# Inverting the chunk matrix of delta attention on diagonal tiles of the PE array

## The chip, the core and the metric

The kernel runs on one core of a Trainium2 chip, in one launch. The metric is device time in microseconds (us). The core's engines work at the same time, each in the order of its own queue: TensorE (PE, matmuls, with PEld for the loading of weights), VectorE (DVE), ScalarE (ACT), GpSimd (POOL) and SyncE (SP), whose queue issues the DMAs. Matmul results arrive in PSUM and must be copied out by DVE or ACT.

## What is computed

The reference is two transformer layers on 2 x 1,024 tokens of width 512, all in float32. The part that matters here is the attention of the first layer, a gated delta rule with 6 heads of 64:

```python
def step(S, inputs):
    q_t, k_t, v_t, g_t, b_t = inputs
    S = S * jnp.exp(g_t)[..., None, None]
    kv = jnp.einsum('bhk,bhkv->bhv', k_t, S)
    u = b_t[..., None] * (v_t - kv)
    S = S + jnp.einsum('bhk,bhv->bhkv', k_t, u)
    o_t = jnp.einsum('bhk,bhkv->bhv', q_t * scale, S)
    return (S, o_t)
```

The kernel doesn't run this step by step. It takes the tokens in chunks of 128. Inside a chunk the updates `u` of all 128 tokens solve a triangular system, one per head: a 128x128 matrix with ones on its diagonal, which holds the weighted products of the keys. The kernel inverts this matrix for each chunk and head. There are 8 chunks per batch, so 16 inversions of 6 matrices each. After the attention come an MLP with 4-bit weights, a second attention and a second MLP with 2:4 sparsity.

## The kernel before

The class `Delta` does the first attention. Batch 0 runs in `first`, batch 1 in `second`. For each chunk there are four streams of instructions, written as Python generators; each `yield` ends a step.

- `prepare(c)` (6 steps) makes the keys, the decay and the matrix. It keeps the matrix transposed as `AT` (128 partitions x 6 heads x 128). At its end `gather` (L603, L605) sends the eight 16x16 blocks on the diagonal to DRAM and back as one tile of 48 x 16 x 16.
- `solve(c)` (5 steps) inverts these 48 blocks on DVE, row by row (L617, L618). ACT turns the result round (L621). Two DMAs (L625) write both forms to DRAM, and twelve DMAs read them back: eight of 16x16 blocks (for 6 heads) into `X16` (L628), four into `T16` (L631), the transposed form of the even blocks.
- `invert(c)` (8 steps) makes the whole inverse `X` out of the small ones by doubling: with the two diagonal blocks of a pair inverted, the block off the diagonal is minus one inverse times the block of the matrix times the other inverse. It goes from 16 to 32 to 64 to 128. In the first two levels each head is one 128x128 matmul, with everything off the blocks zero: the product with `AT` (L644), a masking by `signs` into `mix` on DVE (L646), the product of `mix` and `X` (L654), an ACT copy (L656). `mix` holds the identity in its odd blocks. Then the transposed even blocks are needed for the next level; PE makes them by a transpose (L661 after level one, L670 after level two), and ACT copies them into `Te` (L663, L672). The last level takes two products of 64x64 tiles (L676, L682), whose results DVE moves (L678, L683).
- `advance(c)` (7 steps) uses `X` and the state: it computes `u` (L703), the output and the next state, and ends with a transpose (oT, L758) and the output projection (out_ps or, in the second batch, small_ps at L201).

In `first` each slot of the loop has 24 ticks. A stream gets a length and a range of ticks, and its steps are spread evenly over them. In one slot run `advance` of a chunk, `invert` of the next, `solve` of the one after that, `prepare` of the third, and the projections of later chunks, in this program order within a tick.

In `second` a slot runs three streams together: `normed`, `late` (`invert`, then `advance` of chunk slot - 1) and `early` (`prepare` of chunk slot, two empty steps, `solve`). Each round takes one step of each stream that is not yet done and yields `fill`, 3.3 us. For every yield `weave` puts in steps of the first MLP (`mlp[0].rest()`, lines L1042 and L201 with o_ps) until their nominal 3.4 us each have used up what is due. What is left of the MLP when `second` ends runs after it without interruption. So a slot lasts as many rounds as its longest stream needs, and one more in which the streams are found to be over.

The order of PE, DVE, ACT and POOL is the program's order, under `tc.manual_schedule`. The order of SP, and so of the DMA issues, is not among the engines listed there.

PSUM has three pools: `one` (two tiles of one bank), `two` (two tiles of two banks, called `wide` here) and `acc` (two single banks, taken in turn by `small`). `AT`, `X`, `Te`, `mix` have one buffer each, except `AT` with three (first batch) or two; `X16` and `T16` have one.

```python
streams = [normed(slot - 2), late(slot - 1), early(slot)]
while streams:
    streams = [f for f in streams if next(f, self) is not self]
    yield fill
```

Of the kernel before, what the change touches and what calls it, by code (L numbers as in the profile page):

```python
# [26 lines left out]
F32 = mybir.dt.float32  # L27
# [4 lines left out]
ALU = mybir.AluOpType  # L32
# [4 lines left out]
P = 128  # L37
# [5 lines left out]
NH, DH = 6, 64  # L43
# [109 lines left out]
def bc(ap, shape):  # L153
    return ap.to_broadcast(shape)
# [94 lines left out]
SB = 16  # L249
# [4 lines left out]
class Delta:  # L254
# [36 lines left out]
    def tools(self):  # L291

        core, nc, a = self.core, self.core.nc, self.a
        wp = core.pools("d_w")
        self.wo = wp.tile([P, NG, DM], F32, name="wo0")
        nc.sync.dma_start(out=self.wo, in_=a["wo0"])

        self.upper = wp.tile([P, P], F32, name="upper")
        nc.gpsimd.memset(self.upper, 1.0)
        nc.gpsimd.affine_select(  # L300
            out=self.upper, in_=self.upper, pattern=[[1, P]], compare_op=ALU.is_ge, fill=0.0, base=0,
            channel_multiplier=-1,
        )
        self.ones = wp.tile([P, P], F32, name="ones")
        nc.gpsimd.memset(self.ones, 1.0)


        self.signs, self.mix = {}, {}
        for w in (SB, 2 * SB):
            n = P // (2 * w)  # L310
            sg = wp.tile([P, n, w], F32, tag=f"signs{w}", name="signs")
            nc.gpsimd.memset(sg, -1.0)
            for pattern, base, mult in (
                ([[-2 * w, n], [0, w]], -w, 1),
                ([[2 * w, n], [0, w]], 2 * w - 1, -1),
            ):
                nc.gpsimd.affine_select(
                    out=sg, in_=sg, pattern=pattern, compare_op=ALU.is_ge, fill=0.0, base=base,
                    channel_multiplier=mult,
                )  # L320
            nc.gpsimd.affine_select(
                out=sg, in_=sg, pattern=[[-2 * w, n], [-1, w]], compare_op=ALU.not_equal, fill=1.0, base=0,
                channel_multiplier=1,
            )
            self.signs[w] = sg
            m = wp.tile([P, NH, P], F32, tag=f"mix{w}", name="mix")
            nc.gpsimd.tensor_copy(m, bc(core.ident[:, None, :], [P, NH, P]))
            self.mix[w] = m

        self.X16 = wp.tile([P, NH, P], F32, name="X16")  # L330
        nc.gpsimd.memset(self.X16, 0.0)
        self.T16 = wp.tile([P, NH, P // 2], F32, name="T16")
# [154 lines left out]
    def prepare(self, c):  # L487
# [79 lines left out]
        pT = self.ring("pT", [P, NH, P], keep)  # L567
        AT = self.ring("AT", [P, NH, P], deep)
        spots = [self.wide() for _ in range(2)]
        for m in range(NG):  # L570
            for r in range(2):
# [7 lines left out]
                )  # L579
        for i, t in ((1, AT), (0, pT)):  # L580
            for k, ps in enumerate(spots):
# [26 lines left out]
    def solve(self, c):  # L608

        nc, d, inv = self.core.nc, self.d[c], self.inv  # L610
        blk = d.pop("blk")
        n = NB * NH
        turned = inv.rearrange("b s u -> b u s")
        for rows in (range(1, 7), range(7, 11), range(11, 14), range(14, 16)):
            for t in rows:
                prod = self.ring("prod", [n, SB * SB], 1)[:, : t * t].rearrange("b (u s) -> b u s", u=t)
                nc.vector.tensor_mul(prod, turned[:, :t, :t], bc(blk[:, None, :t, t], [n, t, t]))  # L617
                nc.vector.tensor_reduce(inv[:, t, :t], prod, AX.X, ALU.add, negate=True)  # L618
            yield
        invT = self.ring("prod", [n, SB * SB], 1).rearrange("b (s t) -> b s t", s=SB)  # L620
        nc.scalar.copy(invT, turned)  # L621
        names = [f"d{x}{self.b}_{c}" for x in "TX"]
        away = [self.core.tc.dram_tile([NB, NH, SB, SB], F32, name=x) for x in names]
        for t, dst in zip((inv, invT), away):
            nc.sync.dma_start(out=dst.rearrange("n h s t -> (n h) s t"), in_=t)  # L625
        for i in range(NB):
            rows = slice(i * SB, (i + 1) * SB)
            nc.sync.dma_start(out=self.X16[rows, :, rows], in_=away[1][i].rearrange("h s t -> s h t"))  # L628
            if i % 2 == 0:
                cols = slice(i // 2 * SB, (i // 2 + 1) * SB)  # L630
                nc.sync.dma_start(out=self.T16[rows, :, cols], in_=away[0][i].rearrange("h s t -> s h t"))  # L631
        yield

    def invert(self, c):


        nc, ident, d = self.core.nc, self.core.ident, self.d[c]
        AT = d.pop("AT")
        hw = P // 2
        X, Te = self.X16, self.T16  # L640
        for w in (SB, 2 * SB):
            ps = self.small()
            for h in range(NH):
                nc.tensor.matmul(ps[:, h * hw : (h + 1) * hw], AT[:, h, :], Te[:, h, :], start=True, stop=True)  # L644
            mix = self.mix[w]
            nc.vector.tensor_mul(  # L646
                mix.rearrange("p h (i two c) -> p h i two c", two=2, c=w)[:, :, :, 0, :],
                ps[:, : NH * hw].rearrange("p (h i c) -> p h i c", h=NH, c=w),
                bc(self.signs[w][:, None, :, :], [P, NH, hw // w, w]),
            )  # L650
            yield
            ps = self.wide()
            for h in range(NH):
                nc.tensor.matmul(ps[:, h * P : (h + 1) * P], mix[:, h, :], X[:, h, :], start=True, stop=True)  # L654
            X = self.ring("X32", [P, NH, P], 1) if w == SB else self.ring("X", [P, NH, P], 1)
            nc.scalar.copy(X.rearrange("p h t -> p (h t)"), ps[:, : NH * P])  # L656
            yield
            if w == SB:
                ps = self.wide()
                for h in range(NH):  # L660
                    nc.tensor.transpose(ps[:, h * P : (h + 1) * P], X[:, h, :], ident)  # L661
                Te = self.ring("Te", [P, NH, hw], 1)
                nc.scalar.copy(  # L663
                    Te.rearrange("p h (i c) -> p h i c", c=2 * w),
                    ps[:, : NH * P].rearrange("p (h i two c) -> p h i two c", two=2, c=2 * w, h=NH)[:, :, :, 0, :],
                )
            else:
                ps = self.small()
                for h in range(NH):
                    nc.tensor.transpose(ps[:hw, h * hw : (h + 1) * hw], X[:hw, h, :hw], ident[:hw, :hw])  # L670
                Te = self.ring("Te", [P, NH, hw], 1)[:hw]
                nc.scalar.copy(Te.rearrange("p h t -> p (h t)"), ps[:hw, : NH * hw])  # L672
            yield
        ps = self.small()
        for h in range(NH):
            nc.tensor.matmul(ps[hw:, h * hw : (h + 1) * hw], AT[:hw, h, hw:], Te[:, h, :], start=True, stop=True)  # L676
        Y = self.ring("Te", [P, NH, hw], 1)
        nc.vector.tensor_scalar_mul(Y[hw:].rearrange("p h t -> p (h t)"), ps[hw:, : NH * hw], -1.0)  # L678
        yield
        ps = self.small()  # L680
        for h in range(NH):
            nc.tensor.matmul(ps[:hw, h * hw : (h + 1) * hw], Y[hw:, h, :], X[hw:, h, hw:], start=True, stop=True)  # L682
        nc.vector.tensor_copy(X[:hw, :, hw:], ps[:hw, : NH * hw].rearrange("p (h t) -> p h t", h=NH))  # L683
        d["X"] = X
        yield

# [82 lines left out]
    def first(self, xT, weights, mlp):  # L769
# [3 lines left out]
        core, nc, banks, a = self.core, self.core.nc, self.banks, self.a  # L773
# [4 lines left out]
        n = 2  # L778
# [24 lines left out]
        for slot in range(-ahead, CH + 1):  # L803
            streams = []

            def add(stream, length, start=0, end=24):
                streams.append([stream, length, 0, start, end])
# [9 lines left out]
            f = slot + ahead  # L817
# [1385 lines left out]
```

## Time and profile before

| | us |
|---|---|
| three runs | 3,094.76, 3,098.05, 3,098.5; median 3,098.05 |
| the profiled execution's own time | 3,102.61 |
| its span, from the first instruction to the last | 3,100.6 |
| granted PE clock, mean | 0.990 |

| stretch | what runs | PE, DVE, ACT busy us of 100 |
|---|---|---|
| 100 to 200 us | first batch of the delta attention, projections of the second | 92.47, 78.78, 56.82 |
| 300 to 400 us | the same, later, with the first MLP | 94.72, 64.71, 40.72 |
| 400 to 500 us | end of the first batch, first MLP | 98.11, 30.64, 14.22 |
| 600 to 700 us | second batch of the delta attention, first MLP | 97.17, 65.50, 23.76 |
| 1,100 to 1,200 us | its end and the rest of the first MLP | 97.72, 50.79, 15.89 |

Rows of `invert` in the trace, each x16 chunks: L644 makes 24 records per chunk (384 in all), L654 24, L661 6, L670 6, L676 12, L682 12. On DVE: L646 at 550 ns twice per chunk, L678 560, L683 543. On ACT: L656 at 799 ns twice, L663 480, L672 472.

How to read it: a line of the page gives line, engine, operation, what it writes and reads, shapes, count, then busy us in all and mean ns of one. A matmul's form `64*64 64x64` is rows and columns of the array in use, then partitions and elements of what streams through. One f32 matmul call makes two MATMUL records. The busy time of overlapping records counts once in the sum, so the sum divided by the count can be below the duration of one. In the chain of waits each piece has its start, its length, and what PE or another engine did in it; the start of the next piece is the end of this one.

### The profile page before, as it was taken

The numbers are of one execution on the slowest core, as the hardware profiler recorded it, in microseconds if no ns is written. First come the engines' busy times: TensorE is split into PE (matmuls) and PEld (weight loads), VectorE is DVE, ScalarE is ACT, GpSimd is POOL, SyncE is SP. The second block draws the span as 40 slices with busy tenths as digits, with TensorE's granted clock in tenths as the row PEclk, the third lists the DMA queues.
The fourth block names the chain that finished last, engine by engine and source line by source line (L and its number), as shares of the span: only waits on it lengthen the run. The fifth ranks groups of instructions, "written<-read, shape, count | busy, mean of one in ns | idle before, by whom it ended". The sixth has DMA issues, their size and how long they took to land.

```text
span 3100.6 us, 35161 instructions
## 1 busy us (share of the span) xinstructions
PE 3016.1 (97%) x12652; PEld 1583.6 (51%) x12652; DVE 1914.2 (62%) x3554; ACT 961.1 (31%) x1488; POOL 697.5 (22%) x772
## 2 busy tenths in 40 slices
PE   8999999999999999999999999999999999999998
PEld 6777754555555554545435444446433243234547
DVE  6788633565666544477567656745675577354767
ACT  6654311222222211211462125522113511532221
POOL 2223101122222212465221221222002500530000
PEclk9999999999999999999999999999999999999999
DMA  4232313233232225155111110141010010024211
GB/s 138 66 85 66 100 44 111 65 97 98 98 96 82 91 93 171 52 184 199 36 50 63 51 62 26 36 146 58 24 41 1 31 51 14 1 94 144 83 37 51
DMA packets 196525, 235.36 MB, mean 76 GB/s; under 512 B 53952, under 2 KB 148672, under 8 KB 195840
## 3 DMA queue, kind: packets, MB, share of 16 engines
q1 hardware_dynamic: 196352, 233.12, 23.3%
q8 instruction: 100, 1.64, 0.2%
q14 instruction: 73, 0.60, 0.1%
HBM read 160.42 MB, written 72.61 MB: 75 GB/s over the span
## 4 chain that ended last, share of the span: by engine, by line
PE 80%; DVE 9%; POOL 3%; issue 3%; DMA 2%; ACT 1%; SPq 0%; DVEq 0%; POOLq 0%; ACTq 0%
PE z_ps L1042 24%; PE o_ps L201 12%; PE z_ps L1088 8%; PE u_ps L201 5%; PE g_ps L201 5%; PE st_ps L1605 5%; PE av_ps L1636 4%; PE s_ps L1547 4%; DVE cv L475 2%; PE proj_ps L201 1%; DVE prod L617 1%; PE wide_ps L654 1%; PE small_ps L644 1%; PE den_ps L1658 1%; DVE inv L618 1%
## 5 line engine op out<-in xcount | busy, mean ns | idle before, releaser
L1015 ACT COPY part<-z_ps 128x512 f32<-128x512 f32 x288 | 168.7, 586 | 722.4 <-PE z_ps L1042 494.6
L1042 PE MATMUL z_ps<-xT,z_left 128*128 128x512 f32 x768 | 359.4, 597 | 0.1
L1556 DVE TENSOR_REDUCE top<-s_ps 128x2 f32<-128x1024 f32 x256 | 300.9, 1217 | 76.3 <-PE s_ps L1547 76.2
L1042 PE MATMUL z_ps<-xt,z_left 128*128 128x512 f32 x576 | 274.2, 598 | 2.2 <-issue 1.0
L1616 ACT ACTIVATE es<-st_ps 128x1024 f32<-128x1024 f32 x214 | 209.9, 1022 | 125.6 <-PE st_ps L1605 120.4
L1042 PEld LDWEIGHTS z_ps<-xT,z_left 128*128 128x128 f32 x768 | 141.4, 190 | 186.8 <-issue 161.7
L201 PE MATMUL o_ps<-w_down,h 128*128 128x512 f32 x512 | 230.1, 598 | 0.6 <-DVE part L1076 0.6
L1042 PE MATMUL z_ps<-xT,w_left 128*128 128x512 f32 x384 | 180.8, 600 | 4.7 <-DVE part L1076 2.4
L1076 DVE TENSOR_TENSOR part<-z_ps,part 128x512 f32<-128x512 f32 x108 | 74.4, 689 | 178.6 <-PE z_ps L1042 172.9
L1042 PEld LDWEIGHTS z_ps<-xt,z_left 128*128 128x128 f32 x576 | 106.0, 190 | 146.8 <-issue 124.0
L1651 POOL TENSOR_TENSOR es<-es 128x512 f32<-128x512 f32 x96 | 132.6, 1409 | 143.6 <-PE av_ps L1636 139.9
L1605 PE MATMUL st_ps<-q,kT 17*128 17x512 f32 x1024 | 160.1, 650 | 1.8 <-ACT es L1616 1.8
L1547 PE MATMUL s_ps<-kT,q 16*128 16x512 f32 x1024 | 153.9, 640 | 4.9 <-DVE top L1556 4.8
L201 PEld LDWEIGHTS o_ps<-w_down,h 128*128 128x128 f32 x512 | 94.8, 191 | 108.1 <-issue 104.2
L201 PE MATMUL proj_ps<-xT,wqkv 128*128 128x256 f32 x576 | 135.5, 390 | 8.4 <-ACT raw L459 6.7
L1636 PE MATMUL av_ps<-es,v 128*32 128x512 f32 x1024 | 139.2, 615 | 0.0
L1042 PE MATMUL z_ps<-xt,w_left 128*128 128x512 f32 x288 | 136.4, 596 | 1.6 <-DVE part L1076 1.6
L1678 DVE TENSOR_TENSOR acc<-acc,es 128x1024 f32<-128x1024 f32 x96 | 131.8, 1420 | 0.0
L1077 POOL TENSOR_TENSOR h<-h,part 128x512 f32<-128x512 f32 x48 | 66.5, 1388 | 278.9 <-DVE part L1076 278.9
L201 PEld LDWEIGHTS proj_ps<-xT,wqkv 128*128 128x128 f32 x576 | 109.8, 195 | 27.2 <-ACT raw L459 8.9
L1060 DVE TENSOR_TENSOR h<-z_ps,part 128x512 f32<-128x512 f32 x84 | 57.9, 689 | 103.8 <-PE z_ps L1042 90.5
L1206 DVE TENSOR_TENSOR x<-x,o_ps 128x512 f32<-128x512 f32 x64 | 43.8, 685 | 120.0 <-PE o_ps L201 119.8
(317 smaller groups left out, 5177.6 us busy)
## 6 DMA issues: line engine op xcount, KB each, us to landing
sums<-factor SPq DMA_DIRECT2D x24, 512.0 KB, 3.3
kept_gate<-w_left SPq DMA_DIRECT2D x12, 896.0 KB, 3.8
kept_up<-w_left SPq DMA_DIRECT2D x12, 896.0 KB, 3.9
z_left<-kept_gate SPq DMA_DIRECT2D x12, 896.0 KB, 4.6
z_left<-kept_up SPq DMA_DIRECT2D x12, 896.0 KB, 4.6
wd<-kept_down SPq DMA_DIRECT2D x16, 512.0 KB, 4.5
xl<-park SPq DMA_DIRECT2D x32, 256.0 KB, 3.4
z_left<-sums SPq DMA_DIRECT2D x16, 512.0 KB, 4.1
```

What stands on the lines that cost most here:

```text
L201: nc.tensor.matmul(ps, lhsT, rhs, start=(i == 0), stop=(i == len(pairs) - 1))
L1015: self.core.nc.scalar.copy(t, src)
L1042: self.core.nc.tensor.matmul(ps, left[l][:, k, :], self.right[r][:, k, :], start=(first and k == 0), stop=(k == 1), skip_group_check=True,)
L1076: nc.vector.tensor_add(v, ps, v)
L1088: nc.tensor.matmul(ps[:, i * dm : (i + 1) * dm], left[l][:, k, i * P : (i + 1) * P], right[r][k], start=(first and i == 0 and k == 0), sto ...
L1547: nc.tensor.matmul(tiles[h4 // 2][:, h4 % 2 * 512 : h4 % 2 * 512 + 512], q1s[t][r : r + HALF, gr, :], kT[r : r + HALF, gr, j * 512 : (j + ...
L1556: nc.vector.tensor_reduce(top[:, j, h : h + 2], tiles[e].rearrange("p (i k) -> p i k", i=2), AX.X, ALU.max, negate=True)
L1605: nc.tensor.matmul(tiles[h4 // 2][h4 % 2], kT[r : r + CR, gr, kt * P : (kt + 1) * P], q2[r : r + CR, gr, :], start=True, stop=True,)
L1616: nc.scalar.activation(t.rearrange("p i q -> p (i q)"), tile[2], AF.Exp, scale=HALF**-0.5)
L1636: nc.tensor.matmul(av[gr][32 * h4 : 32 * h4 + 32, :], v[:, kt, 4 * gr + h4, :], es[u][h4 // 2][:, h4 % 2, :], start=(kt == 0), stop=(kt == ...
L1651: eng.tensor_add(t, t, es[u][h4 // 2][:, h4 % 2, :])
L1678: nc.vector.tensor_add(t, es[u - 1][e] if kt == 1 else t, es[u][e])
```

## The change

`invert` is rewritten in six steps, and works on diagonal tiles of the array instead of full 128x128 products. At the first level the low half (partitions 0 to 63) and the high half (64 to 127) are separate 64x64 matmuls, on 64 columns of a compact `X16` (128 x 6 x 64). At the second level only the 32x32 blocks that are not known yet are computed, on 32x32 tiles. The transposed forms are no longer made by PE transposes: the same product is computed again with its two operands exchanged (`pt` beside `ps`). `X` is one of two tiles taken in turn, with its lower left quarter set to zero once; the copies write only the blocks. `solve` loads into the compact tiles, with the same twelve DMAs. The set-up in `tools` keeps one `signs` and one `mix` of 64 columns in place of two of 128. In `first`, the stream's length goes from 8 to 6.

```diff
+        self.Xs = [wp.tile([P, NH, P], F32, name=f"X{i}") for i in range(2)]
+        for X in self.Xs:
+            nc.gpsimd.memset(X[hw:, :, :hw], 0.0)
...
-            nc.sync.dma_start(out=self.X16[rows, :, rows], in_=away[1][i].rearrange("h s t -> s h t"))
+            cols = slice(i % 4 * SB, (i % 4 + 1) * SB)
+            nc.sync.dma_start(out=self.X16[rows, :, cols], in_=away[1][i].rearrange("h s t -> s h t"))
             if i % 2 == 0:
-                cols = slice(i // 2 * SB, (i // 2 + 1) * SB)
+                cols = slice(i % 4 // 2 * SB, (i % 4 // 2 + 1) * SB)
                 nc.sync.dma_start(out=self.T16[rows, :, cols], in_=away[0][i].rearrange("h s t -> s h t"))
...
+        ps = heads(self.small()[:, : NH * qw])
         for h in range(NH):
+            for part in halves:
+                nc.tensor.matmul(ps[part, h, :], AT[part, h, part], self.T16[part, h, :], start=True, stop=True)
+        mix = self.mix
+        nc.vector.tensor_mul(
+            mix.rearrange("p h (i two c) -> p h i two c", two=2, c=SB)[:, :, :, 0, :],
+            ps.rearrange("p h (i c) -> p h i c", c=SB),
+            bc(self.signs[:, None, :, :], [P, NH, 2, SB]),
+        )
         yield
+        wide = self.wide()
+        ps, pt = (heads(wide[:, o : o + NH * hw]) for o in (0, 512))
         for h in range(NH):
+            for part in halves:
+                nc.tensor.matmul(ps[part, h, :], mix[part, h, :], X16[part, h, :], start=True, stop=True)
+        for h in range(NH):
+            for part in halves:
+                nc.tensor.matmul(pt[part, h, :], X16[part, h, :], mix[part, h, :], start=True, stop=True)
+        for part in halves:
+            nc.scalar.copy(X[part, :, part], ps[part])
+        Te = self.ring("Te", [P, NH, hw], 1)
+        nc.scalar.copy(Te, pt)
+        yield
+        ps = heads(self.small()[:, : NH * qw])
+        for h in range(NH):
+            for p in range(2):
+                e, o = quarters[2 * p : 2 * p + 2]
+                nc.tensor.matmul(ps[o, h, :], AT[e, h, o], Te[e, h, :qw], start=True, stop=True)
+        Z = self.ring("Z", [P, NH, qw], 1)
+        for o in quarters[1::2]:
+            nc.vector.tensor_scalar_mul(Z[o], ps[o], -1.0)
+        yield
+        ps = heads(self.small()[:, : NH * qw])
+        pt = heads(self.small()[:, : NH * qw])
+        for h in range(NH):
+            for p in range(2):
+                e, o = quarters[2 * p : 2 * p + 2]
+                nc.tensor.matmul(ps[e, h, :], Z[o, h, :], X[o, h, o], start=True, stop=True)
+        o = quarters[1]
+        for h in range(NH):
+            nc.tensor.matmul(pt[o, h, :], X[o, h, o], Z[o, h, :], start=True, stop=True)
+        for p in range(2):
+            e, o = quarters[2 * p : 2 * p + 2]
+            nc.scalar.copy(X[e, :, o], ps[e])
+        o = quarters[1]
+        nc.scalar.copy(Te[o, :, :qw], pt[o])
+        yield
+        ps = heads(self.small()[:, : NH * hw])
+        for h in range(NH):
+            nc.tensor.matmul(ps[high, h, :], AT[low, h, high], Te[low, h, :], start=True, stop=True)
+        Y = self.ring("Y", [P, NH, hw], 1)
+        nc.vector.tensor_scalar_mul(Y[high], ps[high], -1.0)
+        yield
+        ps = heads(self.small()[:, : NH * hw])
+        for h in range(NH):
+            nc.tensor.matmul(ps[low, h, :], Y[high, h, :], X[high, h, high], start=True, stop=True)
+        nc.vector.tensor_copy(X[low, :, high], ps[low])
         d["X"] = X
         yield
...
             if 0 <= slot + 1 < CH:
-                add(self.invert(slot + 1), 8, 4)
+                add(self.invert(slot + 1), 6, 4)
```

Here `low` and `high` are the two halves of the partitions, `quarters` the four quarters, `hw` is 64, `qw` 32, and `SB` 16.

More of the change, by code (lines that the diff above doesn't have):

```diff
@@ L305, in tools @@
         nc.gpsimd.memset(self.ones, 1.0)
[L308 to L320, printed above, removed]
+        hw = P // 2
@@ L321, in tools @@
+        sg = wp.tile([P, 4, SB], F32, name="signs")
+        nc.gpsimd.memset(sg, -1.0)
+        for pattern, base, mult in (
+            ([[-2 * SB, 4], [0, SB]], -SB, 1),
+            ([[2 * SB, 4], [0, SB]], 2 * SB - 1, -1),
+        ):
             nc.gpsimd.affine_select(
-                out=sg, in_=sg, pattern=[[-2 * w, n], [-1, w]], compare_op=ALU.not_equal, fill=1.0, base=0,
-                channel_multiplier=1,
-            )
-            self.signs[w] = sg
-            m = wp.tile([P, NH, P], F32, tag=f"mix{w}", name="mix")
@@ L327, in tools @@
-            nc.gpsimd.tensor_copy(m, bc(core.ident[:, None, :], [P, NH, P]))
-            self.mix[w] = m
-        self.X16 = wp.tile([P, NH, P], F32, name="X16")
+                out=sg, in_=sg, pattern=pattern, compare_op=ALU.is_ge, fill=0.0, base=base, channel_multiplier=mult
+            )
+        nc.gpsimd.affine_select(
+            out=sg, in_=sg, pattern=[[-2 * SB, 4], [-1, SB]], compare_op=ALU.not_equal, fill=1.0, base=0,
+            channel_multiplier=1,
+        )
+        self.signs = wp.tile([P, 2, SB], F32, name="signs_half")
@@ L331, in tools @@
+        self.mix = wp.tile([P, NH, hw], F32, name="mix")
+        for p in range(2):
+            rows = slice(p * hw, (p + 1) * hw)
+            nc.gpsimd.tensor_copy(self.signs[rows], sg[rows, 2 * p : 2 * p + 2])
+            nc.gpsimd.tensor_copy(self.mix[rows], bc(core.ident[rows, None, rows], [hw, NH, hw]))
+        self.X16 = wp.tile([P, NH, hw], F32, name="X16")
         nc.gpsimd.memset(self.X16, 0.0)
-        self.T16 = wp.tile([P, NH, P // 2], F32, name="T16")
+        self.T16 = wp.tile([P, NH, 2 * SB], F32, name="T16")
@@ L634, in invert @@
     def invert(self, c):
[L637 to L673, printed above, removed]
@@ L674, in invert @@
-        ps = self.small()
-        for h in range(NH):
-            nc.tensor.matmul(ps[hw:, h * hw : (h + 1) * hw], AT[:hw, h, hw:], Te[:, h, :], start=True, stop=True)
-        Y = self.ring("Te", [P, NH, hw], 1)
-        nc.vector.tensor_scalar_mul(Y[hw:].rearrange("p h t -> p (h t)"), ps[hw:, : NH * hw], -1.0)
+        nc, d = self.core.nc, self.d[c]
+        AT, X, X16 = d.pop("AT"), self.Xs[c % 2], self.X16
+        hw, qw = P // 2, P // 4
+        low, high = slice(0, hw), slice(hw, P)
+        halves = (low, high)
@@ new lines, in invert, with heads @@
+        quarters = [slice(i * qw, (i + 1) * qw) for i in range(4)]
+        def heads(ap):
+            return ap.rearrange("p (h t) -> p h t", h=NH)
+        ps = heads(self.small()[:, : NH * qw])
+        for h in range(NH):
+            for part in halves:
[5 more added lines that the diff above has]
+            bc(self.signs[:, None, :, :], [P, NH, 2, SB]),
+        )
@@ L679, in invert @@
         yield
-        ps = self.small()
+        wide = self.wide()
+        ps, pt = (heads(wide[:, o : o + NH * hw]) for o in (0, 512))
         for h in range(NH):
-            nc.tensor.matmul(ps[:hw, h * hw : (h + 1) * hw], Y[hw:, h, :], X[hw:, h, hw:], start=True, stop=True)
-        nc.vector.tensor_copy(X[:hw, :, hw:], ps[:hw, : NH * hw].rearrange("p (h t) -> p h t", h=NH))
+            for part in halves:
+                nc.tensor.matmul(ps[part, h, :], mix[part, h, :], X16[part, h, :], start=True, stop=True)
@@ new lines, in invert @@
+        for p in range(2):
+            e, o = quarters[2 * p : 2 * p + 2]
[9 more added lines that the diff above has]
+        yield
```

## The prediction

> **What bounds the kernel now.** I read the page's busy line first, then busy time by windows, then the chain of waits piece by piece for the two stretches in which `invert` runs (chunks 0 to 7 of the first batch, its L644 rows from 112 to 428 us, and of the second, 545 to 1,128 us).
>
> ```profile
> PE 3016.1 (97%) x12652; PEld 1583.6 (51%) x12652; DVE 1914.2 (62%) x3554; ACT 961.1 (31%) x1488; POOL 697.5 (22%) x772
> ```
> ```profile
> 200.00:300.00 100.00, 93.79 (x570) 74.41 (x569) 84.07 (x236) 51.70 (x98) 26.14 (x32) 1.00 0.25 69
> ...
> 700.00:800.00 100.00, 97.76 (x405) 55.58 (x404) 58.21 (x127) 28.03 (x48) 24.08 (x27) 1.00 0.32 105
> ```
> The first figures behind the window are busy us of PE, PEld, DVE, ACT, POOL. From 200 to 300 us DVE is nearly as full as PE; from 700 to 800 us only PE is. The chain's pieces, added by engine, say the same: from 100 to 300 us 94 us are DVE and 42 PE; from 300 to 450 us 120 of 150 are PE; from 500 to 1,150 us 572 of 650 are PE. So a us of PE work is worth a us in the second batch, about that in the last three chunks of the first, and little before them.
>
> **What `invert` costs now.** One chunk in the chain, between matmul blocks of eight 128x512 records:
>
> ```profile
> 1103.92 3.43 PE o_ps L201 x8
> 1107.35 1.28 PE small_ps L644 x12
> 1108.64 3.49 PE o_ps L201 x8
> ...
> 1116.90 0.45 PE small_ps L670 x6
> 1117.35 3.63 PE o_ps L201 x8
> 1120.98 0.84 PE small_ps L676 x12
> ```
> The reader is to see two things. One f32 matmul makes two records, a transpose one. And a block of eight takes 3.43 us beside full-array work but 3.63 between two visits to 64x64 tiles (L670, L676), so a visit costs 0.20 us beside its own 0.84: PE pays for changing the tile size. The starts of L676's records lie 58 ns apart, 0.70 for twelve. Per chunk: L644 twice 2.56, L654 twice 2.68, L661 0.66 (1.34 and 0.66 in the same view), L670 0.45 + 0.20, L676 and L682 1.04 each. Sum **8.63 us**, 138 us for 16 chunks.
>
> **What it costs after.** Six visits, all on small tiles: 24, 48, 24, 36, 12 and 12 records, 156 for 84. One after another, at 58 ns for a 64-column record (L676) and about half, 30 ns, for a 32-column one (an estimate by columns; bounds 15 and 58) plus 0.34 for each visit (1.04 - 0.70): 1.73 + 3.12 + 1.06 + 1.42 + 1.04 + 1.04 = 9.41. That is 0.8 more than now. The change pays only if the records of the low and the high half, which alternate in program order, run side by side. The trace of before has no pair of diagonal tiles, but neighbours:
>
> ```profile
> 573.42 0.47 PE L670 MATMUL small_ps<-ident,X 64*64 64x64 f32 x5
> 573.67 0.48 PE L573 MATMUL wide_ps<-tmp,qkT 64*128 64x256 f32 x1
> 573.72 0.22 PE L670 MATMUL small_ps<-ident,X 64*64 64x64 f32 x1
> 573.78 1.51 PE L573 MATMUL wide_ps<-tmp,qkT 64*128 64x256 f32 x11
> ```
> ```profile
> L1636 PE MATMUL av_ps<-es,v 128*32 128x512 f32 x1024 | 139.2, 615 | 0.0
> ```
> L573 alternates between the two row halves: 12 records of 256 columns take 1.5 us, where 16 records of the same width on the full array (L201 proj_ps, 228.05 to 231.71 in the chain) take 3.66, so twelve would take 2.75. It runs in pairs. Its first record even starts before the last L670: the other row half goes ahead. L1636 puts four column tiles into one PSUM bank: 139.2 / 1,024 = 0.14 us a record of 512 columns, against 0.43 (3.43 / 8) on the full array. So pairs by rows and by columns both work, and I take the pair on the diagonal at full overlap: 24 x 0.029 + 0.34 = 1.04; 48: 1.73; 24 of 32 columns in pairs 0.36 + 0.34 = 0.70; 36, of which 24 pair, 0.72 + 0.34 = 1.06; then 1.04 twice. Sum **6.61**, 2.0 less per chunk: 16 us in each batch where PE binds. Bounds: 9.41 with no overlap; with it 6.1 and 7.6 for the two ends of the 32-column record.
>
> The Trainium skill speaks against it: "TensorEngine Tiling (Array Packing)", Gotcha 1, says that different row tiles can't use one PSUM bank at the same time, and here low and high share a bank (on other partitions). L573 keeps its halves in separate banks, so no row here refutes it for row tiles; L1636 does for column tiles. By the rule the sum would be 9.41, by the rows 6.61.
>
> Evictions. DVE: two of 128x384 (0.55 each, L646) become one of 128x192 and two of 32x192 (0.35 each, an estimate from L730, 64x192 at 348 ns); L678 and L683 stay: 2.2 us before, 2.15 after. ACT: two of 0.80 (L656), 0.48 and 0.47 become three of about 0.47 (L672's shape) and three of about 0.3: 2.55 to 2.3. Nothing gained or lost on DVE where it binds. POOL's set-up shrinks by some 3 us, at 2 to 7 us and 465 to 488 us, beside PE work: nothing. X gets a second buffer: I find no wait on it, nothing.
>
> **The price that the diff doesn't show.** `invert` yields six times, not eight. In the first batch its steps are only spread wider over the same 24 ticks. In the second a slot lasts as many rounds as its longest stream: 8 + 7 + 1 = 16 now, 14 after, as `early` (6 + 2 + 5 yields) needs 14 too. Each round brings one block of MLP matmuls; those that go come back after the last slot (the MLP runs on to 1,200 us), so they cost nothing. But they cover the way of `solve`'s result through DRAM. `solve` sends its blocks in round 13; the next slot's round 1 reads T16:
>
> ```profile
> 608.39 7.13 PE z_ps L1042 x16
> 615.52 0.33 PE small_ps L758 x3
> 615.85 3.44 PE z_ps L1042 x8
> 619.29 2.58 PE small_ps L201 x6
> 621.86 6.87 PE z_ps L1042 x16
> 628.73 1.28 PE small_ps L644 x12
> ```
> ```profile
> 616.34 0.37 SPq L625 DMA_DIRECT2D dT<-inv  x1
> ...
> 623.36 0.43 SPq L631 DMA_DIRECT2D T<-dT  x1
> ```
> ACT's copy (L621) ends at 612.95 and L644 starts 15.6 us later. After the change oT and out_ps (0.33 + 2.58) lie ahead of that copy and two blocks (6.87) are gone: 15.6 - 9.8 = 5.8 us remain. The last T16 load is issued at 623.36 and lands 1.6 later (median of L631), at about 625 = copy + 12. L644, with every later PE instruction and their DVE and ACT readers queued behind it, would wait some 6 us. In chunk 9 SP is held up by eight L938 loads before L625. The other chunks, by the same rows (gap left; T16 landed, after the copy): chunk 10 5.5; 11.5. 11 8.7; 7.3. 12 6.6; 15.5 (SP held by kept_gate and seven L938). 13 3.8; 8.3. 14 6.9; 7.2. 15 6.3; 6.7. Waits 6 + 6 + 0 + 9 + 4.5 + 0.3 + 0.4 = **26 us** if SP's order stays. Chunk 8 already has only two blocks there (5.4 us) and doesn't wait, because SP sends the four T16 loads ahead of X16: landed 4 us after the copy; that order in all slots costs **0**. SP's queue isn't in the hand-written order, so the order after is open. I take a prompt queue with mixed loads, the nearest to chunks 11, 14 and 15: T16 at copy + 7.5, against gaps of 3.8 to 8.7: about 2 us x 7 = **14**.
>
> **Sum.** Second batch -16 + 14 = -2. First batch: 2.0 for the last three chunks, and a quarter of it (the part of `invert` that lies on the chain there, 9 of some 43 us) for five: -6 - 2 = -8; bounds 0 and -16. Together **-10 us**. The profiled execution took 3,102.6 us (span 3,100.6), 4.6 above the median of 3,098.05; I take the difference off the median: **3,088 us**.
>
> **Rivals.**
> 1. Forecast, chance 0.38: pairs overlap, T16 comes about 2 us late in seven slots. -10, from -17 to -4; own range 3,081 to 3,094.
> 2. T16 in time, 0.27: SP sends T16 first, as for chunk 8. -16 - 8 = -24: **3,074**; with all of the first batch's 16, 3,066. For: that slot has the same two blocks. Against: in six of the other seven slots a load of X16 or several lie between.
> 3. T16 as late as now, 0.17: -24 + 26 = +2: **3,100**; slower as soon as waits pass 30 us, 4.3 per slot. For: SP waits 47 us for DVE w_left at L934 between 590 and 1,140 us. Against: two of those delays are rows of MLP loads, which become fewer per slot.
> 4. The slower one, 0.18: low and high don't overlap. Place: the first four visits. Price: 9.41 - 8.63 = 0.8 per chunk, 6 in the second batch and some 3 in the first, plus the 14 of T16: +23, **3,121**. Without T16's wait it decides where less than 0.28 of the overlap comes (0.8 / 2.8). Against it stand L573 and L1636. That the change doesn't do what it says is this case.
>
> About 0.2% (6 us) is what a measurement of this kernel can tell from no change. Faster by more: 0.33 of case 1 and case 2, 0.60. Within: 0.05 of case 1, 0.13 of case 3, 0.18. Slower: 0.04 of case 3, case 4, 0.22. The range leaves out half of case 4 and the fringe of 2: **3,070 to 3,114**.
>
> **What would show it.** In the timeline, low and high records of step 1 starting within some 10 ns and the 24 ending within about 0.8 us (right), or 1.4 (case 4). Step 2 in about 1.5 us. A block between two visits still at 3.63. In the waits of PE after 590 us, step 1 waiting for T or a semaphore for about 2 us per slot (case 1), none (2) or 4 and more (3). L573 and L676 unchanged. Slots of 68 instead of 77 us. The forecast is wrong most easily in SP's order, which I can't read from before, and in how much of the first batch DVE paces.

## The result, and the profile after

The changed kernel takes 3,126.66 us (median of five runs, 3,122.35 to 3,129.11), against 3,098.05 before: a ratio of 1.0091, interval 1.0077 to 1.0105. It is 28.6 us **slower**; the forecast was 10 us faster, and the time lies above the range. The profiled execution took 3,122.35 us (span 3,120.3), the fastest of the five, so the two profiles differ by 19.7 us and not by 28.6.

Line numbers have moved. In the new kernel `solve` is L619 and L620 on DVE, its copy on ACT L623, its loads L631 and L634; the six steps of `invert` start at L653, L665 (with L668), L678, L688 (with L691), L700 and L706; oT is L782 (758 before), fed by R (L778); the MLP's blocks are L1066 and o_ps at L201. The line of busy time on the page:

```profile
PE 3000.9 (96%) x13804; PEld 1544.1 (49%) x13804; DVE 1920.9 (62%) x3570; ACT 958.8 (31%) x1520; POOL 696.3 (22%) x772
```

PE is busy 15 us less than before (3,016.1), in a longer span. So the work did shrink, and PE waits more. By windows (busy us of PE, PEld, DVE, ACT, POOL with counts, then granted clock, DMA share, GB/s):

```profile
200.00:300.00 100.00, 93.19 (x767) 71.65 (x766) 83.86 (x239) 55.00 (x108) 26.80 (x31) 0.98 0.20 57
...
600.00:700.00 100.00, 85.79 (x400) 45.66 (x400) 56.03 (x125) 22.54 (x41) 19.43 (x24) 0.90 0.29 90
700.00:800.00 100.00, 93.10 (x581) 51.82 (x582) 58.37 (x128) 30.48 (x57) 24.86 (x29) 0.98 0.33 107
```

From 600 to 700 us PE was busy 97.17 us before and is now busy 85.79, at a clock of 0.90. The steps of `invert` themselves are as short as forecast. In the chain of waits, one chunk:

```profile
855.05 0.84 PE wide_ps L665 x24
855.89 0.70 PE wide_ps L668 x24
...
863.66 0.50 PE small_ps L678 x24
864.16 3.63 PE z_ps L1066 x8
```

Step 2's 48 records take 1.54 us, step 3's 24 take 0.50, and the block behind a visit to small tiles takes 3.63 as before. What PE now waits for, in the view of waits from 540 to 1,140 us (us in all, times, longest), starts with two lines of which the view of before has none:

```profile
PE small_ps L653 <- DMA T<-dT: 18.2, 7, 6.4
PE small_ps L782 <- DVE R L778: 10.7, 4, 4.6
```

The first is the wait for T16 that the prediction priced at 14 us: seven waits, in five of the seven slots. The second is oT, the end of `advance`, which waits for DVE. The chain from 815 to 852 us shows both in one slot:

```profile
830.27 0.77 DVE prod L619
831.07 0.25 DVE inv L620
831.32 0.59 DVE x L1230
831.91 0.85 DVE R L778
832.76 0.14 issue
832.90 0.88 PE small_ps L782 x3
833.77 5.57 PE o_ps L201 x8
...
847.79 1.70 DMA T<-dT
849.49 0.14 issue
849.62 0.85 PE small_ps L653 x22
```

R stands in DVE's queue behind rows of `solve` and the MLP's own work (x); PE stood idle for 4.58 us ahead of L782, and the block behind it took 5.57 us instead of 3.43, as the granted clock was 0.5 from 831 to 838 us. Before, the same place is PE alone, as the prediction's lines from 608 to 630 us show. Two rounds fewer per slot move `advance` up against `solve`: its last steps, oT and the output projection (before in rounds 14 and 15, behind all of `solve`), now fall into rounds 12 and 13, and R into round 11, while `solve` does its rows in rounds 9 to 12.

They also bring the end of `solve` closer to the next `invert`. T16 is read from dT, and dT is written from `inv`, DVE's own result; only dX needs ACT's copy. So T16's way begins with DVE's last row. By the timelines, in the seven slots from 590 us on that row (L620) ends 8.3 to 12.6 us before L653's turn comes, on average 10.4; in e1 below it is 13.8 to 19.3, on average 17.1. The 6.7 us between them are about the two blocks that went (6.87).

The other part is SP's queue. Nearly half of the 18.2 us (6.39 and 2.46) lies in one slot, at 620 us, where the last row had ended 12.6 us ahead:

```profile
613.88 0.43 SPq L627 DMA_DIRECT2D dT<-inv  x1
614.41 0.37 SPq L627 DMA_DIRECT2D dX<-prod  x1
614.83 0.42 SPq L882 DMA_DIRECT2D gw<-gw  x1
621.95 0.35 SPq L958 DMA_DIRECT2D codes<-in_pk_down  x1
...
622.87 0.38 SPq L634 DMA_DIRECT2D T<-dT  x1
```

SP issues dT late, behind loads for the MLP, and then stands for 6.6 us at L958, a load of MLP codes that waits for DVE; the loads of T16 stand behind it. Such waits are longer than before. SP's own waits from 590 to 1,140 us, first before, then after:

```profile
SPq L934 <- DVE w_left L953: 47.0, 8, 12.9
```
```profile
SPq L958 <- DVE w_left L977: 85.1, 12, 14.0
```

The balance closes with PE alone. The stretch is from chunk 8's first matmul of `invert` to the first matmul of the second attention (lat_ps). "Half clock" is the time in which the granted clock is 0.5.

| kernel | stretch, us | PE busy | PE waits | half clock |
|---|---|---|---|---|
| before | 692.3 | 674.7 | 17.4 | 10.2 |
| after | 721.3 | 671.3 | 50.2 | 47.8 |
| e1, two empty steps between `invert` and `advance` | 678.5 | 656.0 | 22.2 | 6.8 |
| e2, two empty steps behind `advance` | 694.9 | 662.6 | 32.2 | 24 |
| e3, before with `solve` two steps later | 734.5 | 686.9 | 47.4 | 51 |
| e9, one empty step ahead of `invert`, one behind | 667.7 | 651.9 | 15.8 | 10.2 |

Waits grow by 32.8 us. Busy time falls by only 3.4, though e1, with the same matmuls, is busy 18.7 less than before: the other 15.3 us are nearly all the same work at half the clock, at which PE worked 35.2 us here and 6.8 in e1.

The stretch grew by 29.0 us, more than the 19.7 between the two profiles. Chunk 8 starts 5.9 us earlier after the change (540.0 against 545.9 us), and what follows the stretch is 3.4 us shorter. The earlier start is no finding: among the profiles of kernels with the same first batch it lies between 540.0 and 546.4.

How a stall costs twice is seen in windows of 3.4 us:

```profile
619.80:623.20 3.40, 0.00 (x0) 0.00 (x0) 3.00 (x7) 0.00 (x0) 0.19 (x1) 0.96 0.03 11
623.20:626.60 3.40, 0.39 (x2) 0.28 (x2) 0.00 (x0) 0.00 (x0) 1.21 (x2) 0.50 0.33 79
626.60:630.00 3.40, 1.15 (x21) 1.19 (x22) 0.00 (x0) 0.00 (x0) 0.00 (x0) 0.50 0.16 29
630.00:633.40 3.40, 3.40 (x16) 2.71 (x14) 1.31 (x3) 0.81 (x1) 0.00 (x0) 0.54 0.18 57
```

PE waits at L653 from 619.6 to 626.0 us. In the window without any work the granted clock (third figure from the end) is still near 1; then it drops to 0.5 and stays there through the first window that is full again, 630 to 633.4, whose work is done at about half speed.

### The profile page after: what moved, and what is told of

It reads as the page before. It is cut to its first block, busy times and chain, and to the rows that moved or that the text cites. A ratio compares the mean times of both kernels' runs of the same rounds, so it can differ in the third digit from the quotient of the medians.

```text
span 3120.3 us, 37545 instructions
## 1 busy us (share of the span) xinstructions
PE 3000.9 (96%) x13804; PEld 1544.1 (49%) x13804; DVE 1920.9 (62%) x3570; ACT 958.8 (31%) x1520; POOL 696.3 (22%) x772
## 4 chain that ended last, share of the span: by engine, by line
PE 79%; DVE 11%; DMA 3%; issue 2%; POOL 2%; SPq 1%; ACT 1%; DVEq 0%; POOLq 0%; ACTq 0%
PE z_ps L1066 24%; PE o_ps L201 11%; PE z_ps L1112 8%; PE u_ps L201 5%; PE g_ps L201 5%; PE st_ps L1629 5%; PE s_ps L1571 4%; PE av_ps L1660 4%; DVE cv L477 2%; DVE prod L619 1%; DVE inv L620 1%; PE den_ps L1682 1%; PE proj_ps L201 1%; PE hT_ps L1474 1%; PE wide_ps L527 1%
## 5 line engine op out<-in xcount | busy, mean ns | idle before, releaser
L1066 PE MATMUL z_ps<-xT,z_left 128*128 128x512 f32 x768 | 359.3, 597 | 0.1
L1066 PE MATMUL z_ps<-xt,z_left 128*128 128x512 f32 x576 | 274.2, 598 | 2.2 <-issue 1.0
L201 PE MATMUL o_ps<-w_down,h 128*128 128x512 f32 x512 | 233.8, 608 | 1.8 <-DVE x L1230 1.0
L1066 PEld LDWEIGHTS z_ps<-xT,z_left 128*128 128x128 f32 x768 | 141.4, 190 | 186.8 <-issue 161.7
L1066 PE MATMUL z_ps<-xT,w_left 128*128 128x512 f32 x384 | 181.8, 603 | 7.7 <-DVE h L1084 3.1
L1066 PEld LDWEIGHTS z_ps<-xt,z_left 128*128 128x128 f32 x576 | 106.0, 190 | 146.8 <-issue 124.1
L201 PEld LDWEIGHTS o_ps<-w_down,h 128*128 128x128 f32 x512 | 97.2, 195 | 116.1 <-issue 110.2
L1066 PE MATMUL z_ps<-xt,w_left 128*128 128x512 f32 x288 | 140.5, 611 | 3.8 <-DVE part L1100 2.7
L201 PE MATMUL proj_ps<-xT,wqkv 128*128 128x256 f32 x576 | 137.0, 391 | 7.4 <-ACT raw L461 7.3
L1702 DVE TENSOR_TENSOR acc<-acc,es 128x1024 f32<-128x1024 f32 x96 | 131.8, 1420 | 0.0
L201 PEld LDWEIGHTS proj_ps<-xT,wqkv 128*128 128x128 f32 x576 | 109.0, 194 | 27.7 <-ACT raw L461 10.9
```

What stands on the lines that cost most here:

```text
L201: nc.tensor.matmul(ps, lhsT, rhs, start=(i == 0), stop=(i == len(pairs) - 1))
L1066: self.core.nc.tensor.matmul(ps, left[l][:, k, :], self.right[r][:, k, :], start=(first and k == 0), stop=(k == 1), skip_group_check=True,)
L1702: nc.vector.tensor_add(t, es[u - 1][e] if kt == 1 else t, es[u][e])
```

## The experiments

Theory A is the place: two rounds fewer per slot bring the end of `advance` onto DVE beside `solve`'s rows, and `solve`'s end close to the next `invert`. Its rivals are that one of these two does it alone (the load of T16, or the meeting on DVE), and that the narrow matmuls themselves cost more than their rows show. Unless it is said otherwise an edit is one of the changed kernel, in `second`.

**e1: the two rounds given back, between `invert` and `advance`.**

```diff
                 yield from self.invert(c)
+                yield
+                yield
                 yield from self.advance(c, keep)
```

> The changed kernel with two empty steps between invert and advance in the second batch, so that a slot again lasts 16 rounds and advance, solve and the loads of T16 stand to each other as before. Theory A (the loss comes from the two rounds that are gone: T16 late, and waits of PE for DVE at the oT transpose, each with half-clock windows behind it): PE waits for T16 near 0, the second batch is 16 us faster than before, 3,070 to 3,082 in all, granted clock back to 0.99. Theory B (the narrow tiles themselves lower the granted clock, or cost PE more than their records show): clock stays near 0.98, 3,105 or more.

3,080.13 us beside 3,099.83 for the kernel before: ratio 0.9938 (0.9925 to 0.9950), 19.7 us faster. The chain of e1 at the same place of a slot, a slot later, is PE without a gap:

```profile
917.48 0.33 PE small_ps L782 x3
...
922.11 6.87 PE z_ps L1068 x16
928.97 0.82 PE small_ps L653 x24
```

So the narrow tiles pay, and the whole loss and more (48 us between e1 and after, each against the kernel before) is the place.

**e2: the two rounds given back behind `advance`.** `solve`'s result gets its cover of two blocks again, but the end of `advance` still meets `solve`'s rows.

```diff
                 yield from self.advance(c, keep)
+                yield
+                yield
```

> The changed kernel with the two empty steps behind advance: 16 rounds, four blocks of cover for T16 again, but advance still runs two rounds early against solve. If T16 alone makes the loss: 3,075 to 3,085, no wait at oT above 2 us in the second batch. If the meeting of advance's end with solve on DVE counts too: T16 waits near 0 but about 10 us of waits at oT stay, with their half-clock windows, 3,090 to 3,105. Theory B: 3,105 or more.

3,098.33 us, ratio 0.9996 (0.9987 to 1.0005). That is 18.2 us behind e1. In the waits of PE from 540 to 1,140 us the lines of oT and T16 are now

```profile
PE small_ps L782 <- DVE R L778: 7.0, 4, 3.9
...
PE small_ps L653 <- DMA T<-dT: 2.2, 1, 2.2
```

The kernel as changed differs from e2 only in the two rounds behind `advance`, above all in T16's cover. It loses another 30.1 us there (each against the kernel before it was run beside): T16's wait goes from 2.2 to 18.2 us and half clock from 24 to 48. So the meeting on DVE costs 18 us by itself, and taking the cover away as well costs 30 more.

**e4: the copy held back.** e1, with `solve`'s last step (its copy and 14 DMAs) held back by two rounds. It was meant to test the short cover alone, without the meeting on DVE.

```diff
-                yield from self.solve(c)
+                steps = self.solve(c)
+                for _ in range(4):
+                    next(steps)
+                    yield
+                yield
+                yield
+                yield from steps
```

> The first of these kernels (two empty steps between invert and advance), with the last step of solve, the copy and its 14 DMAs, held back by two rounds: DVE's order against advance as before, only T16's cover is short. If T16 is the larger part: waits for T16 of 15 to 26 us and half-clock windows, 3,095 to 3,110. If the meeting on DVE is the larger part: waits below 10 us, 3,080 to 3,090. Theory B: 3,120 or more.

3,090.96 us, ratio 0.9971 (0.9961 to 0.9981), 10.8 us behind e1. The waits, same view:

```profile
PE z_ps L1074 <- DVE h L1092: 9.7, 3, 7.7
...
PE small_ps L653 <- DMA T<-dT: 1.4, 2, 0.7
```

T16 is nearly in time, but the edit doesn't do what it was made for. SP doesn't follow the program's order, and dT needs only DVE's last row. In the slot whose copy ends at 619.0 and whose L653 starts at 630.8 us:

```profile
613.06 0.32 SPq L627 DMA_DIRECT2D dT<-inv  x1
614.66 1.25 SPq L634 DMA_DIRECT2D T<-dT  x3
...
625.35 0.38 SPq L627 DMA_DIRECT2D dX<-prod  x1
625.77 0.43 SPq L634 DMA_DIRECT2D T<-dT  x1
```

Three of the four loads of T16 leave before the copy. Over the seven slots the last row ends 14.5 to 19.2 us before L653, as in e1 and not as in the changed kernel. So the copy came late, but T16's cover wasn't short, and no run tests the short cover without the meeting. What costs e4 its 10.8 us stays open; the largest wait that e1 doesn't have is one of an MLP block for DVE, 7.7 us.

**e3: the same loss made in the kernel before.** Old `invert`, old slots of 16 rounds, `solve` two steps later.

```diff
                 yield
                 yield
+                yield
+                yield
                 yield from self.solve(c)
```

> The kernel before, with two more empty steps ahead of solve in the second batch: nothing of the new invert, but the same place of solve against advance and the same two blocks of cover for T16 as in the changed kernel; still 16 rounds. Theory A: slower than before by what the changed kernel lost there beyond its saving, 25 to 45 us: 3,123 to 3,143, with waits for T and at oT and a clock near 0.98. Theory B: within 6 us of 3,098, clock 0.99.

3,146.34 us, ratio 1.0146 (1.0133 to 1.0160): 46.5 us slower, 3 above the range expected, without one of the new narrow tiles, and with the same wait for T16:

```profile
PE small_ps L644 <- DMA T<-dT: 19.5, 4, 6.8
...
PE small_ps L758 <- DVE R L754: 2.6, 3, 1.2
```

oT waits only 2.6 us here, so most of what e3 loses comes with T16, the clock and MLP blocks that wait for DVE (8.7 us for h, 1.8 before). e1 and e3 make the case from both sides: the place costs 48 us with the new `invert` and 46.5 with the old one.

**e5: T16 ahead of X16.** The prediction left SP's order open; here the four T16 loads are written first.

```diff
+        for i in range(0, NB, 2):
+            ...
+            nc.sync.dma_start(out=self.T16[rows, :, cols], in_=away[0][i].rearrange("h s t -> s h t"))
         for i in range(NB):
...
-            if i % 2 == 0:
-                ...
```

> The changed kernel (14 rounds) with the four loads of T16 written ahead of the eight of X16. Were the place of T16 in SP's queue the larger part of its lateness, the 18 us of waits for T would fall to about 5 and the time to 3,100 to 3,112. If solve's rows come late on DVE, behind the end of advance, and the copy with them, the loads have little to gain: 3,115 to 3,127, waits for T still 10 us or more.

3,113.55 us beside 3,100.12, ratio 1.0039 (1.0025 to 1.0052): 15 us of the 28.6 come back. The waits:

```profile
PE small_ps L783 <- DVE R L779: 10.7, 4, 4.6
PE small_ps L654 <- DMA T<-dT: 8.4, 2, 5.9
```

The time lies between the two forecasts. T16's wait falls from 18.2 to 8.4; oT's stays at 10.7 to the last digit. So the two waits have different causes, and the loads' order mends only the one. Of the 8.4, 5.9 are left in the slot at 623 us, where all four loads still stand behind the load of MLP codes at SP.

**e10: less of `solve` on DVE.** Rows 7 to 15 of the 16x16 inverses of the second batch are left out; the rounds stay at 14.

```diff
-            for t in rows:
+            for t in rows if self.b == 0 or rows[0] == 1 else ():
```

> The changed kernel, 14 rounds, but solve in the second batch leaves out its rows 7 to 15 (nine of fifteen pairs of a product and a reduction on DVE); all else, the DMAs too, stays. If the loss comes from DVE, where solve's long rows meet the end of advance and make the copy and the oT transpose late: waits for T below 4 us, at oT below 2 us, 3,072 to 3,090, with two blocks of cover only. If two blocks of cover are too few for the DMAs whatever DVE does: waits for T of 10 us or more, 3,100 to 3,115.

3,094.11 us beside 3,099.88, ratio 0.9978 (0.9969 to 0.9987): 34 us come back, so the rows on DVE are behind most of the loss. The run doesn't separate the two causes: without these rows `solve` also ends earlier, 19.9 to 23.1 us before L653. T16's wait is still 9.0 us and oT's 6.5, more than expected. The 9.0 (6.4 and 2.5) lie in one slot, at 619 us, where the last row had ended 23.1 us ahead and SP sent dT only 2.4 us ahead, then stood at the same load of MLP codes: there SP's queue makes T16 late, not DVE's rows. Why oT still waits stays open.

**e6: four rounds given back.** As e1 with four empty steps, 18 rounds.

```diff
                 yield from self.invert(c)
+                yield
+                yield
+                yield
+                yield
                 yield from self.advance(c, keep)
```

> Four empty steps between invert and advance in the second batch, 18 rounds per slot. If the two that restore 16 rounds already take the meeting on DVE and T16's lateness away, more change nothing as long as the MLP has work left: within 6 us of the kernel with two, 3,074 to 3,086. If spreading goes on to pay, 3,068 or less; if the MLP runs out under the last slots, 3,090 or more.

3,100.58 us, ratio 1.0004 (0.9993 to 1.0015). More room isn't better: it is 20 us behind e1. Near the end, before 1,222 us, an MLP block waits for the load of its operand, as the MLP's blocks were drawn forward by the added rounds (argued, not tested):

```profile
PE z_ps L1070 <- DMA z_left<-kept_gate: 13.6, 1, 13.6
```

**e7 and e8: which batch gains.** The old `invert` stands beside the new one, and `OLD` names the batch that uses it: e7 the first (with 8 steps there, and e1's empty steps in the second), e8 the second.

```diff
     def invert(self, c):
+        return self.invert_old(c) if self.b in self.OLD else self.invert_new(c)
```

> The new invert in the second batch alone, with the two empty steps; the old invert, with 8 steps, in the first batch. If the saving lies in the second batch, where PE paces, and the first gives 0 to 6 us: 3,080 to 3,087. If the first batch gives its 8 us: 3,086 to 3,090.

> The new invert in the first batch alone, the old one in the second: no pads needed. If the first batch, paced by DVE, turns the saved PE time into idle time and half-clock windows: 3,094 to 3,100, within 0.2% of before. If it gains the 8 us that I forecast: 3,088 to 3,092.

e7 3,087.84 us, ratio 0.9958 (0.9946 to 0.9971), 12.3 us faster than the kernel before. e8 3,099.35, ratio 1.0000 (0.9989 to 1.0010): the first batch gives nothing. Why, one window from 112 to 540 us tells, first of before:

```profile
112.00:540.00 428.00, 410.09 (x2153) 287.05 (x2152) 264.54 (x721) 161.96 (x298) 80.74 (x107) 0.99 0.26 79
```

and then of e8:

```profile
112.00:540.00 428.00, 406.57 (x2722) 273.32 (x2720) 263.02 (x731) 160.71 (x313) 81.08 (x106) 0.96 0.27 79
```

PE works 3.5 us less in the same time and waits 3.4 more (17.8 before, 21.2 in e8); the clock falls from 0.99 to 0.96, with some 34 us at half clock instead of 7. The shorter matmuls leave PE waiting, mostly for DVE, and what they save goes into the slower clock. The two gains add up to 13 us, e1's is 19.7; the 7 us between them stay open, and the intervals, 3 to 4 us to each side for each of the three, nearly cover them.

**e9: the empty steps divided**, one ahead of `invert` and one between.

```diff
+                yield
                 yield from self.invert(c)
+                yield
                 yield from self.advance(c, keep)
```

> 16 rounds again, but one empty step ahead of invert and one between invert and advance, in the second batch. Advance stands to solve as before; the second product of invert no longer meets prepare's decay product (L527) in one round, where PE waited 6.5 us in all in the kernel with both steps between. If that wait is worth its length: 3,070 to 3,077. If PE finds another wait in its place: 3,077 to 3,084.

3,077.71 us beside 3,099.88: ratio 0.9931 (0.9918 to 0.9944). This is the fastest version, 22 us below the kernel before and some 50 below the change as made, though not told apart from e1 by its interval. It loses e1's wait of 6.5 us at L527 and gets one of 4.4 at L565. The view names no releaser for L527's wait (six times about 1.08); the likely one is step 2 of `invert`, whose PSUM tile `prepare` would take next: in one slot of e1 ACT's last copy out of it, L672, ends at 712.11 us and L527 starts at 712.21.

**e11: the halves in turn.** e1, with the loops of the first two steps exchanged: all heads of the low half, then all of the high one.

```diff
-        for h in range(NH):
-            for part in halves:
+        for part in halves:
+            for h in range(NH):
```

> The kernel with both empty steps between invert and advance, with the two loops over heads and halves exchanged in the first three products: all six heads of the low half, then all six of the high half. If PE runs the halves side by side only where they alternate in program order: 0.7 + 0.7 + 0.7 us more per chunk, 16 us in the second batch, 3,093 to 3,100, and the records of a half 58 ns apart with the other half behind them. If the queue looks far enough ahead: within 6 us of 3,080.

3,105.19 us, ratio 1.0017 (1.0008 to 1.0027), 25 us above e1 and 5 above the first forecast, with no wait added (20.4 us in the stretch). Step 1 in the timeline (start, us from the first record's start to the last one's end), in e1 and then in e11:

```profile
703.59 0.89 PE L653 MATMUL small_ps<-T,AT 64*64 64x32 f32 x24
```
```profile
706.42 1.38 PE L653 MATMUL small_ps<-T,AT 64*64 64x32 f32 x24
```

Step 1 takes 0.49 us more, and step 2, from the first record of L665 to the last of L668, 2.48 instead of 1.62: 1.35 us per chunk, 11 in the second batch. PE is busy 17 us more in the stretch (673.1); the other 6 are the clock, at half for 20.5 us instead of 6.8. What makes up the rest of the 25 us in the medians isn't shown. So 1.35 of the 2 us that the change saves per chunk hang on the order: the program must alternate low and high to have the full overlap.

## Why the prediction was wrong, step by step

**What bounds the kernel.** Right for the second batch, where PE's busy time and waits add up to the stretch within 0.5 us. Wrong for the last three chunks of the first, which were taken as PE's: e8 gains nothing, and from 300 to 440 us its PE is busy for 131.8 us instead of 134.7, at a clock of 0.95 instead of 0.98: it waits more and runs slower.

**The cost of `invert`.** Right. Forecast 6.61 us a chunk, 2.0 less; e1 is busy 18.7 us less over eight chunks, of which some 1.6 are less time at half clock: 2.1 each. Low and high start 6 to 7 ns apart in step 1, and after 0.82 us PE goes on to the next line. Step 1's records stream only 32 columns but were priced like those of 64, and that was right: a pair starts every 58 ns. The rule that speaks against it, Gotcha 1 of "TensorEngine Tiling (Array Packing)" in the Trainium skill, isn't borne out for halves that share a bank on different partitions. Rival 4, in which they don't overlap, falls; e11 shows what losing a part of the overlap costs.

**Evictions and set-up.** Right: in e1 DVE is busy 1,914.4 us against 1,914.2 before, ACT 959.0 against 961.1.

**The second buffer of X.** Priced at nothing; no run takes it away. Not foreseen is the wait at L527, 6.5 us, against 3.8 at the same line (L525) before.

**T16's wait, +14.** In sum near, 18.2 us, and partly by luck. The working measured from ACT's copy, which T16 doesn't need. It took T16 to land 7.5 us after that copy against gaps of 3.8 to 8.7 us, about 2 us late in each slot. In the trace the gaps are longer, 7.6 to 10.9, and the last load lands later, 7.8 to 20.0 us after the copy; two slots are in time, two lose under 1 us, and the slots at 620 and 1,065 us make 14.6 of the 18.2. The two errors offset each other. The working named SP's order as the open point, and there the largest wait lies; rival 3's sign, SP's wait for w_left, grew from 47.0 to 85.1 us. Of the lower clock behind the waits it had nothing.

**"Each round brings one block of MLP matmuls; those that go come back after the last slot [...], so they cost nothing."** This is the step that failed. The blocks do come back. But the rounds also keep `advance`'s last steps behind `solve`'s rows: oT's 10.7 us of waits were priced at nothing, and the meeting alone costs 18.2 us (e2). The steps that `advance` moves past DVE's queue were never set beside it; for DVE the working asked only whether its evictions cost more. Rows that showed the danger were there: DVE busy 65.5 us of 100 from 600 to 700 us. Nor did a slot shrink to the 68 us forecast: from 626 to 1,068 us it takes 73.7 on average, against 77.1 before.

**The clock isn't in the sum at all.** 15.3 us, nearly as large as the whole gain. The page "TensorE: Matmul & The Clock Gate" of the Trainium skill (Terms, and Part 1) says that an idle window of about 3.4 us halves the clock, and that the loss is the throttled time times one half. The trace agrees on the length: half clock comes in pieces of 3.4, 6.8 and 10.2 us. It agrees on the idle window only in part: in the 3.4 us before the drop at 622.9 us PE worked 0.1 us, but before those at 592.2 and 599.0 us 1.0 and 1.1. By the rule the 41.0 us more at half clock than in e1 would cost 20.5; measured are 15.3, since PE stood idle for 12.6 of the 47.8 us at half clock. The trace of before had a case of it too: 10.2 us at half clock in the same stretch.

**First batch, -8 (bounds 0 and -16).** Measured -0.8 (e8, with 3 us to each side), at the bound: PE waits, mostly for DVE, and is slowed.

**The balance for the second batch**: forecast -16 + 14 = -2. By the profiles -18.7 + 32.8 + 15.3 = +29.4 (the stretch grew by 29.0). Of the 32.8, 18.2 are T16's, 10.7 oT's; the rest are small waits for MLP operands and PSUM.

Left open: what the short cover would cost without the meeting on DVE, how its 30 us divide between the two missing blocks and SP's queue, what e4 lost, and the 7 us between e1 and the sum of e7 and e8.

## What to carry to other kernels

When a change takes steps out of one stream, lay out the new rounds of all streams that run beside it, on every engine, before pricing what was removed: here the steps that went were worth more as spacing (48 us) than the work that they held (19 us). Give the steps back as empty ones and measure; where they stand matters (e2 is 18 us behind e1), and too many lose the gain again (e6). Before holding back a step to test a wait, see in the trace what the awaited DMA itself waits for, and what stands ahead of it in SP's queue. On a bound TensorE price each stall of several us with the slower clock behind it.

## What the runs showed of the hardware

- Two 64x64 tiles on the diagonal of the array run side by side though they write one PSUM bank: 24 records of 32 columns take 0.82 us when the program alternates the tiles (e1), and 1.30 when it does all of one and then all of the other (e11), each to the start of the next line.
- Two 32x32 tiles go at 32 ns a pair of 32-column records: 24 in 0.50 us.
- In a stall of 6.4 us at L653 the granted clock falls to 0.5 after 3.3 us, and stays there for 10.2. Over the second batch, stalls that add 33 us add 15 us more in this way.
